# A convolution's last two groups of tokens: transformed while they are on chip, with two results put aside, instead of stored and loaded again

## The chip, the cores and the metric

The kernel runs on one core of a Trainium2 chip. The metric is the device time of one execution in microseconds (us). Three runs of the kernel before took 985.76, 987.46 and 989.23 us; the median, 987.46 us, is the time before. A profile is taken from one further execution.

The engines are named as in the profile: PE is TensorE's matrix multiplication and PEld its loading of weights, DVE is VectorE, ACT is ScalarE, POOL is GpSimd and SP is SyncE, which here only issues transfers (DMAs). ACTq, SPq and POOLq are the instruction queues of these engines where they issue a DMA. Every engine works through its own instructions in order, so an instruction that waits holds up all that stand behind it on the same engine.

## The reference

The computation is a "macaron" block on 2048 tokens of width 1024: half a feed-forward step, then a step of convolution and block-local attention, then half a feed-forward step again, each on normalised tokens and each added to its input. The change lies in the convolution:

```python
x = L0_attn_inputs                                   # (1, 2048, 1024), float32
x = x + 0.5 * ffn(layernorm(x))                      # router, sign weights
x = x + attn(layernorm(x))
x = x + 0.5 * ffn(layernorm(x))

# at the head of attn:
x = lax.conv_general_dilated(inputs, conv_w, window_strides=(1,), padding='SAME',
        dimension_numbers=('NWC', 'WIO', 'NWC')) + conv_b   # 3 taps, 1024 -> 768 channels
q, k, v = jnp.split(x, 3, axis=-1)                   # each 256 wide, then 16 heads of 64 in blocks of 128
```

## The kernel before

**Stages.** The first feed-forward step runs over 16 tiles of 128 tokens. It ends each tile with the normalised tokens of the next step, which TensorE transposes so that channels lie on partitions. Then comes the convolution, then attention, then the second feed-forward step.

**The convolution in eight points.** Three taps on runs of six outputs are computed with eight products instead of eighteen. From eight neighbouring inputs of each run, VectorE makes eight combinations, the points k = 0 to 7; from the three taps come eight combinations of weights; TensorE multiplies point k of the inputs by point k of the weights; and VectorE turns the eight products of a run into its six outputs. 2048 tokens are 342 runs of six. The tile `V[k]` holds point k of all 342 runs, with 8 chunks of 128 channels (DC = 8), so 8 x 342 columns. `product(w, k, ...)` (L528) multiplies one `V[k]` for one of six output chunks `w` of 128 channels. It is 8 matrix products in float32, which the trace shows as 16 instructions of line 520, and ScalarE copies its result out of the accumulator (L535, L537). Accumulators are four banks that the products take in turn.

**Groups.** Three token tiles make a group: 64 runs, or 512 columns of `V[k]` over the 8 chunks. There are six groups, n = 0 to 5 (TRIPLES = 6); the last has only 22 runs, 176 columns. The tokens of a group lie in a window tile of 1560 KB. There are two window buffers (`xwp`, L90ff.) while the feed-forward step runs. `transpose_x2` (L396) fills them in turn. When a group is complete, `end_transform` (L435, three instructions) makes points 0 and 7 from it, and `store_window` (L444) writes the window to memory outside the chip, since the buffer is wanted for a later group. Groups 4 and 5 are the last two and still lie in the two buffers when the feed-forward step ends. Their store is done in `conv_ends` (L551 to L553).

**Inner points.** Points 1 to 6 come in pairs (1,2), (3,4), (5,6), from `transform(n, k, ...)` (L454): six VectorE instructions for one group and one pair, two each for the sums over even and odd neighbours and two that combine them (L464 to L469). The memory has room for six `V` tiles at a time. So `V[1]` to `V[4]` are made during the products of points 0 and 7, in `conv_ends` (L539), and `V[5]`, `V[6]` take over the buffers of `V[0]` and `V[7]` when the products of these are done, in `last_transforms` (L568). The order of groups in `conv_ends` is the list `jobs` (L543): 4 and 5 from the buffers where they lie, then 0, 1, 2, 3, loaded again by `load_window` (L448) on ScalarE's queue; one transform goes beside each of the twelve products. In `last_transforms` the order is 1, 2, 3, 0, 4, 5, and while it runs the windows 0, 4 and 5 are loaded again. At most three windows are on chip at a time: two in `xwp`, one in `xs`.

**Weights.** The combinations of taps for points 1 to 6 are made by `taps_begin` (L491; loads on GpSimd's queue, one of them adding) and `taps_end` (L504; two VectorE instructions, L508 and L509) for each output chunk and pair. The first product of a pair needs line 508. For the first output chunk, `taps_end` for points 5 and 6 stands behind `last_transforms` (L731 to L733). The pinned instructions (`pin`) keep the order of the program among themselves; all others are put in an order by a planner that runs when the program is built, from estimated costs, and that order is what each engine follows.

**Behind it.** When the windows are done with (`wins.close()`, L732), three attention weights (L745) are loaded by SP into their memory. `outputs` (L583) turns the products of a chunk into the tile `y` (tag `y6`, 342 x 6 columns, one buffer), which is stored; it is first used after the first chunk's last product.

Of the kernel before, what the change touches and what calls it, by code (L numbers as in the profile page):

```python
# [9 lines left out]
F32 = mybir.dt.float32  # L10
# [7 lines left out]
P = 128  # L18
# [6 lines left out]
def kernel(  # L25
# [22 lines left out]
    nc = tc.nc  # L48
# [4 lines left out]
    NT = T // P  # L53
    DC = D // P
    NW = conv_w.shape[0]
# [8 lines left out]
    def pool(stack, name, bufs, **kw):  # L64
        return stack.enter_context(tc.tile_pool(name=name, bufs=bufs, reuse_waits="tile", **kw))

    const = pool(ctx, "const", 1)
    spill = pool(ctx, "spill", 1, space=DRAM)
# [4 lines left out]
    def bank(kind, shape, name):  # L73
        return banks[kind].tile(shape, F32, name=name, tag=kind)
# [14 lines left out]
    xwp = pool(wins, "xwp", 2, side="right")  # L89
# [261 lines left out]
    NK = 8  # L351
    SCALES = (1.0, -2.0 / 9, -2.0 / 9, 1.0 / 90, 1.0 / 90, 1.0 / 180, 1.0 / 180, 1.0)
    PAIRS = ((1, 2), (3, 4), (5, 6))
    QT = 3 * P // 6
    NQ = -(-T // 6)
    TRIPLES = -(-NT // 3)
    SIZES = [min(QT, NQ - n * QT) for n in range(TRIPLES)]
# [7 lines left out]
    ROW = QT + 1  # L365
    LEFT, RIGHT = 5 * ROW - 1, QT
    AT = (LEFT, *(j * ROW for j in range(6)), 1)
    win_dram = [spill.tile([P, DC, 6 * ROW], F32, name=f"win_{n}") for n in range(TRIPLES)]
    x2, x2ns, xws = {}, {}, {}
    V = {k: ve.tile([P, DC, NQ], F32, name=f"v_{k}", tag=f"v{k}") for k in (0, NK - 1)}  # L370

# [4 lines left out]
    def window(n):  # L376
        if n not in xws:
            xws[n] = xwp.tile([P, DC, 6 * ROW], F32, name=f"xw_{n}", tag="xw")
            if SIZES[n] < QT:

                rows6 = xws[n].rearrange("p c (k q) -> p c k q", q=ROW)
                nc.gpsimd.memset(rows6[:, :, :, SIZES[n] - 1 :], 0.0)
            else:
                nc.gpsimd.memset(xws[n][:, :, 2 * ROW - 1 :: ROW], 0.0)
            if n == 0:
                nc.gpsimd.memset(xws[n][:, :, LEFT : LEFT + 1], 0.0)
        return xws[n]
# [8 lines left out]
    def transpose_x2(t):  # L396
        xn = x2ns.pop(t)
        n, third = divmod(t, 3)
        xw = window(n)
        at = third * P  # L400

        head = -at % 6
        tail = (at + P) % 6
        for h in range(DC // 4):
            tr = bank("acc", [P, 4, P], f"tr2_{t}_{h}")
            for c in range(4):
                nc.tensor.transpose(tr[:, c, :], xn[:, ts(4 * h + c, P)], ident)  # L407
            rows6 = xw[:, 4 * h : 4 * h + 4, :].rearrange("p c (k q) -> p c k q", q=ROW)
            q, whole = (at + head) // 6, (P - head - tail) // 6
            copy = nc.scalar.copy  # L410
            copy(
                rows6[:, :, :, ds(q, whole)],
                tr[:, :, head : P - tail].rearrange("p c (q k) -> p c k q", k=6),
            )
            if head:
                copy(rows6[:, :, 6 - head : 6, q - 1], tr[:, :, 0:head])
            if tail:
                copy(rows6[:, :, 0:tail, q + whole], tr[:, :, P - tail : P])
        if third == 2 or t + 1 == NT:
            end_transform(n, 0)  # L420
        if third == 0 and n > 0:
            nc.gpsimd.tensor_copy(xws[n - 1][:, :, RIGHT : RIGHT + 1], xw[:, :, 0:1])
            if t + 1 < NT:
                store_window(n - 1)
        if t == NT - 3:
            window(TRIPLES - 1)
        if third == 2 and n + 1 < TRIPLES:
            nc.gpsimd.tensor_copy(window(n + 1)[:, :, LEFT : LEFT + 1], xw[:, :, LEFT + QT : LEFT + ROW])
    def tokens(xw, n):
        return [xw[:, :, ds(at, SIZES[n])] for at in AT]  # L430

    def columns(k, n):
        return V[k][:, :, ds(n * QT, SIZES[n])]

    def end_transform(n, k, pinned=False):  # L435
        d = tokens(xws[n], n)
        a, b, c, e = (d[0], d[2], d[4], d[6]) if k == 0 else (d[7], d[5], d[3], d[1])
        v = columns(k, n)
        kept = pin if pinned else lambda ins: None
        kept(nc.vector.tensor_tensor(v, c, b, ALU.subtract))  # L440
        kept(nc.vector.scalar_tensor_tensor(v, v, 5.25, a, ALU.mult, ALU.add))
        kept(nc.vector.tensor_tensor(v, v, e, ALU.subtract))  # L442

    def store_window(n, pinned=False):  # L444
        end_transform(n, NK - 1, pinned)
        nc.sync.dma_start(out=win_dram[n], in_=xws[n])

    def load_window(n, pl):  # L448
        xws[n] = pl.tile([P, DC, 6 * ROW], F32, name=f"xl_{n}", tag="xw")
        nc.scalar.dma_start(out=xws[n], in_=win_dram[n])  # L450

    VT = 3

    def transform(n, k, tf):  # L454

        _, d1, d2, d3, d4, d5, d6, _ = tokens(xws[n], n)
        a, b = columns(k, n), columns(k + 1, n)
        tmp = tf.tile([P, DC, QT], F32, name=f"vt_{n}_{k}", tag="vt", bufs=VT)[:, :, 0 : SIZES[n]]
        f, even, odd, last = {
            1: (-4.25, 1.0, 1.0, 1.0),  # L460
            3: (-5.0, 0.25, 4.0, 0.5),
            5: (-1.25, 4.0, 0.25, 2.0),
        }[k]
        nc.vector.scalar_tensor_tensor(a, d4, f, d2, ALU.mult, ALU.add)  # L464
        nc.vector.scalar_tensor_tensor(a, a, even, d6, ALU.mult, ALU.add)
        nc.vector.scalar_tensor_tensor(tmp, d3, f, d1, ALU.mult, ALU.add)
        nc.vector.scalar_tensor_tensor(tmp, d5, odd, tmp, ALU.mult, ALU.add)
        nc.vector.scalar_tensor_tensor(b, tmp, -last, a, ALU.mult, ALU.add)
        nc.vector.scalar_tensor_tensor(a, tmp, last, a, ALU.mult, ALU.add)  # L469
# [69 lines left out]
    def conv_ends(mp, tf, up, xs):  # L539

        jobs = [(TRIPLES - 2, 1, xwp), (TRIPLES - 1, 2, xwp), (0, 3, xs), (1,), (2,), (3,)]  # L543
        load_window(0, xs)
        begun = WORDER[0]
        taps_begin(begun, PAIRS[2], up)
        for at in range(2 * NW):
            last, i = divmod(at, NW)
            w = WORDER[i]
            product(w, last * (NK - 1), gs[w, 2 * last], mp)  # L550
            if at == 0:  # L551
                for n in (TRIPLES - 2, TRIPLES - 1):
                    store_window(n, True)  # L553
            if not last:
                load_g(w, 2)
                if w == begun:
                    taps_begin(w, PAIRS[0], up)
                    taps_begin(w, PAIRS[1], up)
            elif i == 0:
                load_g(w, 1)  # L560
            elif i < 4:
                load_g(WORDER[1], (1, 2, 0)[i - 1])
            n, *more = jobs[at // 2]
            transform(n, 1 + 2 * (at % 2), tf)
            if more and at % 2:
                load_window(*more)

    def last_transforms(tf, xs):  # L568
        for k in PAIRS[-1]:
            V[k] = ve.tile([P, DC, NQ], F32, name=f"v_{k}", tag=f"v{0 if k == 5 else NK - 1}")  # L570
        for n, *more in (
            (1, 0, xwp),
            (2, TRIPLES - 2, xwp),
            (3, TRIPLES - 1, xs),
            (0,),
            (TRIPLES - 2,),
            (TRIPLES - 1,),
        ):
            transform(n, 5, tf)
            if more:  # L580
                load_window(*more)

    def outputs(w, mp):  # L583
        m = ms[w]
# [114 lines left out]
    up = pool(b1, "up", 1)  # L699
    vm = pool(b1, "vm", 1)  # L700
    mp = pool(b1, "mp", 1)
    for k in range(1, 5):
        V[k] = vm.tile([P, DC, NQ], F32, name=f"v_{k}", tag=f"v{k}")
    xs = pool(wins, "xs", 1, side="right")
    tf = pool(wins, "tf", 1, side="right")
    conv_ends(mp, tf, up, xs)
    for ks in PAIRS[:2]:
        taps_end(WORDER[0], ks, up)

# [16 lines left out]
    for i, w in enumerate(WORDER):  # L726
        for ks in PAIRS:
            for k in ks:
                product(w, k, us[w][k], mp)
            if i == 0 and ks[0] == 1:  # L730
                last_transforms(tf, xs)  # L731
                wins.close()  # L732
                taps_end(w, PAIRS[-1], up)  # L733
            if ks[0] == 1 and i + 2 < NW:
                load_g(WORDER[i + 2], 1, 2, 0)
            if i + 1 < NW:
                taps_begin(WORDER[i + 1], ks, up)
            if ks is PAIRS[-1]:
                outputs(w, mp)
            if i + 1 < NW:  # L740
                taps_end(WORDER[i + 1], ks, up)
        if i == 1:
            aw = pool(b2, "aw", 1, side="right")
            qkv0 = pool(b2, "qkv0", 1, side="right")
            wv_sb, wq_sb, wk_sb = (load_rows(aw, a, n, HE) for a, n in ((wv, "wv_sb"), (wq, "wq_sb"), (wk, "wk_sb")))  # L745
# [277 lines left out]
```

## Time and profile before

| what | value |
|---|---|
| median of three runs | 987.46 us (985.76 to 989.23) |
| profiled execution | 990.02 us, span 988.1 us |
| busy share of the span: TensorE, VectorE, ScalarE, GpSimd | 97%, 66%, 41%, 26% |
| window stores (`win<-xw`) | 6 of 1560 KB, median 6.0 us to landing |
| window loads (`xl<-win`) | 7 of 1560 KB, 6.4 to 16.8 us, median 10.1 |
| loads of taps (`u<-in_conv_w_dram`) | 24 of 512 KB, median 5.9 us |
| products of points 0 and 7 | 200.9 to 259.8 us |
| products of points 1 to 6 | 260.1 to 433.8 us |

How to read it: a profile line for a group of instructions names the line of the kernel, the engine, the operation and, as out<-in, the tiles it writes and reads, then the count, the busy time, the mean duration, and the idle time of its engine just before it with what ended that idle time. `xw` is a window as the feed-forward step filled it, `xl` a window loaded again, `win` its copy outside the chip, `vt` the temporary of a transform, `v` a `V` tile, `g` a tap, `u` a combination of taps, `cv` an accumulator, `m` its copy. The shares are averages over the span; what a change inside the convolution does is read from the stretch from 200 to 300 us.

### The profile page before, as it was taken

To read this page: it belongs to the slowest core of one execution; us is meant where nothing else is said; L and a number is where in the kernel's file an instruction comes from. 1 tells how busy PE (TensorE), PEld (TensorE's weight loads), DVE (VectorE), ACT (ScalarE), POOL (GpSimd) and SP (SyncE) were. 2 spreads that over 40 slices of the span, in tenths; PEclk is the share of its full clock that TensorE was granted. 3 is DMA by queue.
4 is the path that set the end of the run, shared out by engine and by line. 5 is a ranking of instruction groups with operands and counts; after the bars stand their busy time and mean duration, and the time that the engine had idled before them with its cause. 6 is when DMAs were issued, how large, how long until landed. Compare 5 with 4: busy or idle time off the path is not lost.

```text
span 988.1 us, 13874 instructions
## 1 busy us (share of the span) xinstructions
PE 959.2 (97%) x5068; PEld 626.9 (63%) x5068; DVE 652.7 (66%) x1229; ACT 407.8 (41%) x1115; POOL 256.0 (26%) x327
## 2 busy tenths in 40 slices
PE   5999999999979999999999999999999999999998
PEld 3778887776646666654555455544554565878776
DVE  4878887786985656735656455645565655777764
ACT  3576665321011111125545344626462572545450
POOL 3554453320001101003303110311031322434331
PEclk9999999999989999999999999999999999999999
DMA  8766753599597675417030241025003236656431
GB/s 251 225 156 195 189 173 129 197 363 363 203 310 202 176 186 122 112 47 283 1 128 1 89 146 43 2 99 199 1 1 107 73 57 192 168 152 163 115 107 64
DMA packets 37396, 143.08 MB, mean 145 GB/s; under 512 B 4361, under 2 KB 5385, under 8 KB 34898
## 3 DMA queue, kind: packets, MB, share of 16 engines
q1 hardware_dynamic: 27760, 101.35, 28.4%
q0 software_dynamic: 8544, 29.64, 15.8%
q10 hardware_dynamic: 1026, 11.22, 3.0%
q8 instruction: 40, 0.66, 0.3%
q14 instruction: 26, 0.21, 0.1%
HBM read 84.37 MB, written 41.04 MB: 127 GB/s over the span
## 4 chain that ended last, share of the span: by engine, by line
PE 49%; issue 31%; DVE 9%; POOL 6%; DMA 4%; ACT 1%; POOLq 0%; SPq 0%; DVEq 0%; ACTq 0%
PE pm_f L287 22%; PE cv L520 11%; POOL xr L798 3%; PE tr_f L200 3%; PE pp L932 2%; DMA xl<-win 2%; POOL p L854 2%; PE lgp_f L208 2%; PE acc L913 2%; PE is_f L251 1%; DMA win<-xw 1%; PE tr L407 1%; PE pq L821 1%; PE ao L896 1%; DVE v L469 1%
## 5 line engine op out<-in xcount | busy, mean ns | idle before, releaser
L287 PE MATMUL pm_f<-sw,y_f 128*128 128x512 f32 x1024 | 265.6, 408 | 0.2 <-DVE x L297 0.2
L287 PEld LDWEIGHTS pm_f<-sw,y_f 128*128 128x128 f32 x1024 | 186.2, 191 | 40.7 <-DVE x L297 0.4
L520 PE MATMUL cv<-v,u 128*128 128x342 f32 x576 | 168.0, 454 | 6.0 <-DVE u L508 6.0
L520 PEld LDWEIGHTS cv<-v,u 128*128 128x128 f32 x576 | 109.8, 191 | 64.2 <-issue 8.2
L854 POOL TENSOR_SCALAR_AFFINE_SELECT p<-p 128x512 f32<-128x512 f32 x64 | 39.7, 645 | 282.9 <-ACT p L852 282.9
L867 ACT ACTIVATE p<-p,anm 128x128 f32<-128x128 f32 x256 | 99.0, 389 | 16.6 <-DVE anm L864 16.6
L265 POOL TENSOR_TENSOR y_f<-xnT_f,y_f 128x512 fp32r<-128x512 f32 x64 | 81.1, 1282 | 59.5 <-ACT y_f L264 58.8
L537 ACT ACTIVATE m<-cv 128x342 f32<-128x342 f32 x42 | 19.1, 456 | 169.7 <-PE cv L520 141.7
L852 ACT COPY p<-sc 128x512 f32<-128x512 f32 x64 | 34.3, 588 | 111.4 <-PE sc L842 111.3
L864 DVE TENSOR_REDUCE anm<-p 128x4 f32<-128x512 f32 x64 | 40.9, 681 | 49.0 <-POOL p L854 49.0
L296 DVE TENSOR_TENSOR pm_f<-pm_f,os_f 128x512 f32<-128x512 f32 x64 | 44.4, 694 | 35.0 <-PE pm_f L287 34.5
L913 PE MATMUL acc<-oT,wo_sb 128*128 128x512 f32 x128 | 67.2, 616 | 0.4 <-DVE oT L905 0.4
L821 PE MATMUL pq<-qkv,wq_sb 128*128 128x512 f32 x128 | 61.0, 596 | 0.0
L821 PE MATMUL pq<-qkv,wk_sb 128*128 128x512 f32 x128 | 60.2, 592 | 0.0
L520 PE MATMUL cv<-v,g 128*128 128x342 f32 (+2 forms) x224 | 57.1, 415 | 0.8 <-DVE v L442 0.8
L932 PE MATMUL pp<-pw_sb,o2T 128*128 128x512 f32 x128 | 57.4, 599 | 0.4
L805 PE MATMUL pv<-wv_sb,qkv 128*128 128x512 f32 x128 | 56.1, 592 | 0.0
L520 PEld LDWEIGHTS cv<-v,g 128*128 128x128 f32 x224 | 39.7, 190 | 17.6 <-DVE v L442 1.2
L201 ACT COPY xnT_f<-tr_f 128x512 f32<-128x512 f32 x60 | 32.6, 589 | 42.0 <-PE tr_f L200 42.0
L508 DVE SCALAR_TENSOR_TENSOR u<-g,u 128x1024 f32<-128x1024 f32 x18 | 22.0, 1224 | 41.5 <-issue 21.6
L867 ACT ACTIVATION_READ_ACCUMULATOR p<-p,anm 128x1 f32 x256 | 48.1, 188 | 0.0
L875 DVE TENSOR_TENSOR p<-p,asum 128x512 f32<-128x512 f32 x64 | 45.6, 712 | 2.2
(141 smaller groups left out, 1484.4 us busy)
## 6 DMA issues: line engine op xcount, KB each, us to landing
g<-in_conv_w_dram SPq DMA_DIRECT2D x28, 512.0 KB, 5.4
u<-in_conv_w_dram POOLq DMA_DIRECT2D x24, 512.0 KB, 5.9
xl<-win ACTq DMA_DIRECT2D x7, 1560.0 KB, 10.1
win<-xw SPq DMA_DIRECT2D x6, 1560.0 KB, 6.0
x<-in_x_dram SPq DMA_DIRECT2D x16, 512.0 KB, 4.5
raw<-in_weight_t_dram SPq DMA_DIRECT2D x16, 512.0 KB, 6.9
x<-hbias POOLq DMA_DIRECT2D x16, 512.0 KB, 5.2
x<-x SPq DMA_DIRECT2D x16, 512.0 KB, 5.1
```

Source lines behind the costliest of these rows:

```text
L265: nc.gpsimd.tensor_tensor(yl, y, yh.bitcast(F32), ALU.subtract)
L287: nc.tensor.matmul(pm, lhsT=y[:, n, c, :], rhs=self.sw[:, c, ts(h, NB)], start=(c == 0 and n == 0), stop=(c == DC - 1 and n == 1),)
L296: nc.vector.tensor_tensor(pm, pm, o, ALU.mult)
L520: nc.tensor.matmul(accs[w, k][:, lo:hi], lhsT=uk[:, c, :], rhs=V[k][:, c, lo:hi], start=(c == 0), stop=(c == DC - 1),)
L805: nc.tensor.matmul(pv, lhsT=qkvs[g][2][:, c, ts(b, P)], rhs=wv_sb[:, c, ts(half, NB)], start=(c == 0), stop=(c == WC - 1),)
L821: nc.tensor.matmul(pq, lhsT=w_sb[:, c, ts(hp, P)], rhs=qkvs[g][n][:, c, :], start=(c == 0), stop=(c == WC - 1),)
L854: nc.gpsimd.affine_select(out=p, in_=p, pattern=[[0, BPG], [-1, P]], compare_op=ALU.is_ge, fill=NEG_INF, base=0, channel_multiplier=1,)
L864: nc.vector.tensor_reduce(nmax, p, AX.X, ALU.max, negate=True)
L867: nc.scalar.activation(p[:, b, :], p[:, b, :], AF.Exp, bias=nmax[:, b : b + 1], accum_out=asum[:, b : b + 1],)
L875: nc.vector.tensor_tensor(p, p, asum.unsqueeze(2).broadcast_to([P, BPG, P]), ALU.mult)
L913: nc.tensor.matmul(accs[g][m], lhsT=wo_sb[:, hp, ts(m, P)], rhs=oT, start=(hp == 0), stop=(hp == NHP - 1),)
L932: nc.tensor.matmul(pp, lhsT=o2T[:, m, ts(b, P)], rhs=pw_sb[:, m, ts(h, NB)], start=(m == 0), stop=(m == WC - 1),)
```

## The change

Windows 4 and 5 are neither stored nor loaded again. All three pairs of inner points of these groups are made in `conv_ends`, while they lie in their buffers. As `V[5]` and `V[6]` have no memory yet, the two results of the third pair go into the tile `kept`, which uses the buffer of `y` (2 x 8 x 86 of its columns; 86 = 64 + 22 runs). `last_transforms` begins with a ScalarE copy of each of the two halves of `kept` into the last 86 runs of `V[5]` and `V[6]`, and then makes only groups 1, 2, 3 and 0. Window 0 is the only one that is loaded a second time, after group 1. The fourteen transforms of `conv_ends` are shared out over its twelve products.

```diff
+    KEPT = (TRIPLES - 2, TRIPLES - 1)
-    win_dram = [spill.tile([P, DC, 6 * ROW], F32, name=f"win_{n}") for n in range(TRIPLES)]
+    win_dram = [spill.tile([P, DC, 6 * ROW], F32, name=f"win_{n}") for n in range(KEPT[0])]
...
         if third == 0 and n > 0:
-            if t + 1 < NT:
+            if n - 1 not in KEPT:
                 store_window(n - 1)
...
-    def transform(n, k, tf):
+    def transform(n, k, tf, into=columns):
-        a, b = columns(k, n), columns(k + 1, n)
+        a, b = into(k, n), into(k + 1, n)
...
     def conv_ends(mp, tf, up, xs):
-        jobs = [(TRIPLES - 2, 1, xwp), (TRIPLES - 1, 2, xwp), (0, 3, xs), (1,), (2,), (3,)]
+        at0 = KEPT[0] * QT
+        y6 = mp.tile([P, NQ, 6], F32, name="kept", tag="y6", bufs=1).rearrange("p q j -> p (q j)")
+        kept = y6[:, 0 : 2 * DC * (NQ - at0)].rearrange("p (k c q) -> p k c q", k=2, c=DC)
+
+        def aside(k, n):
+            return kept[:, k - 5, :, ds(n * QT - at0, SIZES[n])]
+
+        jobs = [
+            *((n, k) for n in KEPT for k in (1, 3, 5)),
+            *((n, k) for n in range(KEPT[0]) for k in (1, 3)),
+        ]
+        loads = {(KEPT[0], 5): (1, xwp), (KEPT[1], 5): (2, xwp), (0, 3): (3, xs)}
         load_window(0, xs)
...
             if at == 0:
-                for n in (TRIPLES - 2, TRIPLES - 1):
-                    store_window(n, True)
+                for n in KEPT:
+                    end_transform(n, NK - 1, True)
...
-            n, *more = jobs[at // 2]
-            transform(n, 1 + 2 * (at % 2), tf)
-            if more and at % 2:
-                load_window(*more)
+            share = len(jobs) * at // (2 * NW), len(jobs) * (at + 1) // (2 * NW)
+            for n, k in jobs[slice(*share)]:
+                transform(n, k, tf, aside if k == 5 else columns)
+                if (n, k) in loads:
+                    load_window(*loads[n, k])
+        return kept

-    def last_transforms(tf, xs):
+    def last_transforms(tf, kept):
         for k in PAIRS[-1]:
             V[k] = ve.tile([P, DC, NQ], F32, name=f"v_{k}", tag=f"v{0 if k == 5 else NK - 1}")
-        for n, *more in ((1, 0, xwp), (2, TRIPLES - 2, xwp), (3, TRIPLES - 1, xs), (0,), (TRIPLES - 2,), (TRIPLES - 1,)):
+            nc.scalar.copy(V[k][:, :, KEPT[0] * QT :], kept[:, k - 5])
+        for n in (1, 2, 3, 0):
             transform(n, 5, tf)
-            if more:
-                load_window(*more)
+            if n == 1:
+                load_window(0, xwp)
...
-    conv_ends(mp, tf, up, xs)
+    kept = conv_ends(mp, tf, up, xs)
...
-                last_transforms(tf, xs)
+                last_transforms(tf, kept)
```

## The prediction

> **What bounds the kernel now.** First the page: span and busy shares, then the group of convolution products.
>
> ```profile
> span 988.1 us, 13874 instructions
> PE 959.2 (97%) x5068; PEld 626.9 (63%) x5068; DVE 652.7 (66%) x1229; ACT 407.8 (41%) x1115; POOL 256.0 (26%) x327
> L520 PE MATMUL cv<-v,u 128*128 128x342 f32 x576 | 168.0, 454 | 6.0 <-DVE u L508 6.0
> ```
>
> TensorE is busy for 97% of the span, so only its gaps and a low clock can be won back by moving other work. In the convolution it is idle for 6.0 us, all of it ended by VectorE's tap combination in line 508. I then asked for the stretches around these gaps (columns: length; busy time and count of PE, PEld, DVE, ACT, POOL; granted clock; DMA share; GB/s).
>
> ```profile
> 204.00:225.60 21.60, 20.75 (x102) 15.72 (x101) 21.58 (x47) 3.99 (x9) 3.25 (x5) 1.00 1.01 355
> 225.60:233.40 7.80, 7.80 (x29) 5.11 (x28) 0.02 (x1) 0.46 (x1) 0.00 (x0) 1.00 1.04 366
> 233.40:259.90 26.50, 26.36 (x92) 17.03 (x90) 26.41 (x43) 2.28 (x5) 0.00 (x0) 1.00 0.67 253
> 259.90:278.90 19.00, 18.67 (x64) 12.04 (x64) 19.00 (x31) 2.31 (x6) 1.41 (x2) 1.00 0.86 315
> 278.90:284.40 5.50, 0.00 (x0) 0.02 (x1) 5.29 (x13) 1.35 (x2) 0.86 (x1) 0.69 1.02 302
> 284.40:287.40 3.00, 2.98 (x6) 1.83 (x6) 2.90 (x3) 0.00 (x0) 0.00 (x0) 0.50 1.07 294
> ```
>
> From 204 to 284 VectorE is full except for one hole, 225.6 to 233.4; TensorE's hole, 278.9 to 284.4, is at the end of the same stretch. Here VectorE sets the pace, and its early hole is paid back as TensorE's late one. The row after it shows a second price: the clock is 0.50 until 287.4. The chain that ended last says what made VectorE's hole (start, length, what):
>
> ```profile
> 208.19 13.71 DMA win<-xw
> 221.91 0.04 ACTq L450
> 221.95 0.04 issue
> 221.99 11.47 DMA xl<-win
> 233.48 0.69 DVE v L464
> ...
> 271.26 8.37 DMA xl<-win
> 279.63 0.02 issue
> 279.65 0.34 DVE v L464
> ```
>
> Group 1 cannot be loaded until group 4, whose buffer it takes, has been stored: 13.71 us of store, then 11.47 us of load. Group 5's reload (8.37 us) is on the chain too, though VectorE waits only 0.17 us for it, because other work fills in. The timeline of TensorE and of the last tap combination closes the picture:
>
> ```profile
> 260.14 18.67 PE L520 MATMUL cv<-v,u 128*128 128x342 f32 x64 [0.38 <-DVE u L508]
> 283.05 1.22 DVE L508 SCALAR_TENSOR_TENSOR u<-g,u 128x1024 f32<-128x1024 f32 x1
> 284.42 16.00 PE L520 MATMUL cv<-v,u 128*128 128x342 f32 x49 [5.61 <-DVE u L508]
> ```
>
> **The change, part by part.** I write (n,k) for the transform of group n for points k and k+1.
>
> *Removed.* Two stores on SP and two reloads on ScalarE's queue (groups 4, 5), 1560 KB each, and with the stores the 13.71 us ahead of group 1's load. SP only issues g loads behind the stores; these may start 0.9 us earlier, worth nothing by itself. ScalarE loses two reload waits on VectorE (at 267.05 and 271.26) that had evictions behind them.
>
> *Moved.* (4,5) and (5,5) go from the tail to the front. A 512-column instruction of VectorE follows another by 0.60 us on the chain, a 176-column one by 0.25 us: 6 x 0.60 + 6 x 0.25 = 5.1 us. They fall where VectorE has its 7.9 us hole. Without that cover the 5.1 us would be neither gain nor loss, since the same 5.1 us leave the tail.
>
> *Added.* Two ScalarE copies of 8 x 86 = 688 columns. No row has this size; ScalarE's 342-column eviction takes 0.456 us and its 1024-column multiply (L501) 1.05, so the line through them gives 0.76 us each. Bounds: 0.59 (the 512-column copy) and 1.05. I take 0.76. The second one waits for V7's buffer, that is for the last k=7 product at 259.6. Behind it on ScalarE stand evictions of the last k=7 and first k=1, 2 products and perhaps the second load of group 0. Four accumulator banks at 4.56 us a product leave an eviction 13.7 us; in the trace one waited 9.96 us behind a window load and TensorE did not stop. Cost: 0; without this cover, each us of ScalarE is one of TensorE.
>
> *VectorE's new sum*, from 204.62 (first end transform of group 4) to the first k=5 taps: ends 5.1; (4,·) and (5,·) with k=1, 3, 5: 3 x 3.62 + 3 x 1.51 = 15.4; (0,1), (0,3) 7.2; six transforms of groups 1 to 3: 21.7; four tap combinations of 1.14: 4.6; (1,5), (2,5), (3,5), (0,5): 14.5; the k=5 taps 1.1. Together 69.6, so 274.2 if nothing waits. The planner ran four 0.43 us instructions of the output step ahead of these taps before; if it does so again, 275.9. (Check on before: 69.6 + 1.7 + the waits 7.86 + 0.17 = 79.3, against 79.65 from 204.62 to 284.27.)
>
> *Do the loads arrive?* Group 1 is issued when (4,5) has read its buffer, about 220.5, and needed when (0,3) is done, 232.3. Before, it took 11.5 us beside two stores: 232.0, no wait. Group 2: issued about 225.1, needed 239.5; between 10.3 and its 16.8 of before, a wait of 0 to 2.8 us. Group 3: needed 246.8, issued 231.7, 10.3: no wait. Group 0 again: issued when (1,5) has read, 261.0, needed 269.5; the load issued at 260.63 before took 7.5 us, the median is 10.1: a wait of 0 to 1.6 us. The Trainium skill ("DMA: Bandwidth & Descriptors", Queues, rings and completion order) speaks against hoping for more: every DMA engine takes the queue rows in turn, packet by packet, so that SP's g loads and POOL's u loads keep halving a window load although the stores are gone. From the page's 358 GB/s and its fixed 2 us I estimate 6.5 us for a load alone and 11 at half rate; the rows (7.5 to 16.8) agree with the second, and I use the rows. Sum of the waits: 0 to 4.4, so VectorE is done between 274.2 and 280.3. I take about 276.5, the nearer end, as each load has slack.
>
> *TensorE.* The last k=7 matmul starts at 259.3; starts are 0.285 us apart, so k=1 can start at 259.6 (its taps are now ready about 255; before, 260.14). Four products are 64 starts, 18.2 us: k=5 is wanted at 277.8. VectorE's 276.5 is earlier, so TensorE doesn't stop. Won: 284.42 - 277.83 = 6.6 us. And the clock: six starts took 2.98 us at 0.50 where 6 x 0.285 = 1.7 would do, 1.3 us. Here a page speaks against me: "TensorE: Matmul & The Clock Gate", Part 1, has a free-running window of about 3.4 us and says of the ramp "don't fit to a specific cold count"; without the 1.3 the gain would be 6.6. I keep it: the row has it in the profiled execution, and where there is no gap there is no ramp to vary. The same page makes a rest of a stall under one window free of clock loss; the trace agrees as far as it goes (the 0.38 us gap at 259.8 left the clock at 1.00).
>
> *Does it last?* From 287 to 988 the waits of TensorE that the profile names add up to 3.5 us, so what follows simply starts earlier. What is late next would be the second output chunk's taps: its u load starts at 268.9 when k=2 is done, a second accumulates (5.3 + 5.9 us, median; up to 13.5 for one), taps 2.3, against a need at 277.8 + 9.1 = 286.9. The three weight loads (1024 KB each) that wait for the windows' memory come at about 272 instead of 275.5 to 286.4 and crowd these u loads, but 3.2 MB of reloads have left the same stretch: 283 to 285, in time.
>
> Sum: 6.6 + 1.3 = 7.9 us. The profiled execution lasted 990.02 us (span 988.1): 982.1. It lay 2.6 us above the median of the runs; on the median, 987.46 - 7.9 = **979.6 us**.
>
> **The rivals.**
>
> *Part of the stall stays.* The waits for groups 2 and 0 add up and the output instructions go first: k=5 starts 1 to 3 us late, at 980.6 to 982.6, and over 3.4 us with the clock's 1.3 on top, up to 984.5. For it: only 1.3 to 3.6 us of slack on VectorE. Against: every load was costed with before's traffic. About 982.
>
> *The hole only moves: no change.* ScalarE issues group 1's load behind an eviction, or the planner puts an instruction that needs a load ahead of work that doesn't, as it did at 233.48 (group 1's first instruction stood ahead of three of (0,3)). Then VectorE idles some 8 us elsewhere and ends at 284 as before: 987. Against: 28 us of VectorE's work now stand ahead of the first needed load.
>
> *Slower: the second load of group 0.* Its place is the end of VectorE's tail, where (0,5) and the k=5 taps, 4.8 us, have to follow it; ScalarE, its issuer, may hold it behind the copy of V6 and an eviction. It decides at a landing of 279.7 (284.42 - 4.8): later than that is slower than before, one for one. Issued at 264.6 behind the k=1 eviction, the longest landing of before (16.8) gives 281.4; behind the k=2 eviction (269.2) it gives 286: 994. With a median landing these are 274.7 and 279.3, still faster. Price taken: about 991.
>
> **How the numbers follow.** Forecast 0.65, part of the stall 0.17, no change 0.08, slower 0.10. Within 0.3% (3 us, about what a measurement of this kernel can tell from no change) lies above 984.5. Faster 0.65 + 0.15 = 0.80; same 0.08 + 0.02 = 0.10; slower 0.10. Range: below, 6.6 + 1.3 plus the 0.85 us that TensorE waits at 209.85 and the spread of the medians (1.7): 977. Above, the partly stalled case with 1 us of spread: 985.5; this leaves out about 0.18 above and little below.
>
> **What would show it.** VectorE's wait for a load of a window falls from 8.0 us to under 3; the store of windows is x4 and the load x5; TensorE has no gap of over 1 us between 204 and 300, and no row at 0.50 there; k=5 of the first chunk starts near 278; the two copies take about 0.76 us. The forecast is wrong if TensorE still waits for line 508 at k=5, if evictions hold it up behind ScalarE's queue, or if the second chunk's taps come late.

## The result, and the profile after

The changed kernel takes 979.38 us (median of six runs, 977.1 to 981.14), the kernel before 986.61 us in six runs beside it. The ratio is 0.9921, with a 95% interval of 0.9894 to 0.9949: 7 us faster. The forecast was 979.6 us. That the two agree to 0.2 us is in part luck: the forecast was taken off a median of three runs, 987.46 us, and six runs have 986.61.

The profiled execution lasted 980.25 us, with a span of 978.0 us. First the page of the kernel after: span, busy shares and the group of the convolution's products, as in the prediction.

```profile
span 978.0 us, 13872 instructions
PE 955.0 (98%) x5068; PEld 624.4 (64%) x5068; DVE 652.0 (67%) x1229; ACT 409.4 (42%) x1117; POOL 256.1 (26%) x327
L521 PE MATMUL cv<-v,u 128*128 128x342 f32 x576 | 166.0, 450 | 0.0
```

The last number of the third line was 6.0 us, ended by the taps of line 508. It is 0.0: nothing stops these products any more. Their mean duration fell from 454 to 450 ns because none of them runs at the low clock. Next the stretches of the same numbers as before; the convolution begins 1.9 us earlier in this execution, so each holds slightly later work (length; busy time and count of PE, PEld, DVE, ACT, POOL; granted clock; DMA share; GB/s).

```profile
204.00:225.60 21.60, 20.75 (x100) 15.39 (x99) 21.57 (x51) 4.11 (x9) 2.46 (x4) 1.00 0.95 276
225.60:233.40 7.80, 7.80 (x29) 5.13 (x28) 7.48 (x13) 1.57 (x3) 0.00 (x0) 1.00 1.01 411
233.40:259.90 26.50, 26.50 (x94) 17.42 (x93) 26.50 (x42) 3.39 (x7) 0.00 (x0) 1.00 0.57 200
259.90:278.90 19.00, 19.00 (x68) 12.49 (x67) 15.40 (x25) 2.86 (x5) 2.27 (x3) 1.00 0.64 213
278.90:284.40 5.50, 5.50 (x21) 3.63 (x20) 3.21 (x4) 0.46 (x1) 0.01 (x1) 1.00 1.04 320
284.40:287.40 3.00, 3.00 (x12) 1.92 (x12) 2.97 (x7) 1.40 (x2) 0.14 (x1) 1.00 1.01 336
```

In the second row VectorE is busy for 7.48 us where it was busy for 0.02. In the fifth TensorE is busy for all of 5.50 us where it did nothing. In the sixth the clock is 1.00 where it was 0.50. The hole has left VectorE and the stop has left TensorE with it. The timeline of the kernel after gives the two instructions that meet there, then the chain of waits what is left of VectorE's wait for a window (total, times, longest):

```profile
257.72 42.49 PE L521 MATMUL cv<-v,u 128*128 128x342 f32 x147
272.52 1.22 DVE L509 SCALAR_TENSOR_TENSOR u<-g,u 128x1024 f32<-128x1024 f32 x1
```

```profile
DVE v L465 <- DMA xl<-win: 0.3, 1, 0.3
```

The products of points 1 to 6 run without a break. The taps that the first k=5 product needs are ready at 273.7. The product wants them 64 starts of 0.285 us after 257.7, at 275.9 (worked out, since no break shows where it starts). So VectorE has 2.2 us to spare.

**Where the time went.** I take as the length of the convolution the time from its first product to the first value product of the attention. It was 433.6 - 201.1 = 232.5 us and is 423.6 - 199.2 = 224.4 us: 8.1 us less. Behind it, both spans have 554.4 or 554.5 us. Ahead of it the two profiled executions differ by 1.9 us, in a stretch that the change doesn't touch. In the execution before, the granted clock was 0.86 from 35 to 40 us and 0.80 from 40 to 45 us, some 3.4 us at half speed and at most 1.7 us lost; in the one after it was 1.00 there. The other versions' profiles, all with the change or most of it, start between 197.7 and 199.6 us. One profile of the kernel before can't show whose these 1.9 us are; that the medians differ by 7.2 us, and the spans, which hold them, by 10.1, speaks against the change.

### The profile page after: what moved, and what is told of

Its sections match the earlier page's. It is cut to its first block, busy times and chain, and to the rows that moved or that the text cites. A ratio compares the mean times of both kernels' runs of the same rounds, so it can differ in the third digit from the quotient of the medians.

```text
span 978.0 us, 13872 instructions
## 1 busy us (share of the span) xinstructions
PE 955.0 (98%) x5068; PEld 624.4 (64%) x5068; DVE 652.0 (67%) x1229; ACT 409.4 (42%) x1117; POOL 256.1 (26%) x327
## 4 chain that ended last, share of the span: by engine, by line
PE 45%; issue 26%; POOL 5%; DVE 1%; DMA 0%; ACT 0%; POOLq 0%; DVEq 0%
PE cv L521 22%; PE pm_f L287 13%; POOL xr L807 3%; PE pp L941 2%; POOL p L863 2%; PE acc L922 2%; PE tr_f L200 1%; PE pq L830 1%; PE lgp_f L208 1%; PE is_f L251 1%; PE ao L905 1%; PE pt L892 1%; PE sc L851 0%; DMA qkv<-y 0%; DVE y L618 0%
## 5 line engine op out<-in xcount | busy, mean ns | idle before, releaser
L521 PE MATMUL cv<-v,u 128*128 128x342 f32 x576 | 166.0, 450 | 0.0
L876 ACT ACTIVATE p<-p,anm 128x128 f32<-128x128 f32 x256 | 99.0, 389 | 16.8 <-DVE anm L873 16.8
```

The source lines that it names most:

```text
L521: nc.tensor.matmul(accs[w, k][:, lo:hi], lhsT=uk[:, c, :], rhs=V[k][:, c, lo:hi], start=(c == 0), stop=(c == DC - 1),)
L876: nc.scalar.activation(p[:, b, :], p[:, b, :], AF.Exp, bias=nmax[:, b : b + 1], accum_out=asum[:, b : b + 1],)
```

## The experiments

The times of one version scatter by several us. The length of the convolution is steadier: the changed kernel and two other versions without a stop, each in one profile, all have 224.4 us. So the experiments are read by that length, by TensorE's stop ahead of the first k=5 product, and by VectorE's waits for windows.

**All four transfers put back, the transforms left where the change put them.**

```diff
...
                 for n in KEPT:
                     end_transform(n, NK - 1, True)
+                    nc.sync.dma_start(out=win_dram[n], in_=xws[n])
...
             if n == 1:
                 load_window(0, xwp)
+            if n == 2:
+                load_window(KEPT[0], xwp)
+            if n == 3:
+                load_window(KEPT[1], xs)
```

> The changed kernel with all four removed transfers put back: the two stores of windows 4 and 5, and in the tail their two loads, which nothing reads. The transforms stay where the change put them. The length of the convolution (first product of point 0 to first value product of the attention) was 232.5 us before and 224.4 us after. Theory A, VectorE's hole is what counted and it now has work to cover it: group 1's load is issued when the stores have landed, about 220 instead of 217.8, VectorE waits 0 to 3 us for it, and its slack of 2.2 us before the k=5 products takes that up: length 224.4 to 225.5, time 979 to 981. Theory B, the traffic of these 6.4 MB slowed the other loads: most of the gain is lost, length 228 to 232.5, time 983 to 987.

Measured: 981.76 us (ratio 0.9918, 0.9887 to 0.9949); length 422.9 - 198.2 = 224.7 us. No stop. The chain of waits of this run:

```profile
DVE v L465 <- DMA xl<-win: 2.3, 1, 2.3
```

Group 1's load waits for the stores again, and VectorE for the load: 2.3 us instead of 0.3. The slack of 2.2 us takes up the 2.0 us more. So it is not the 6.4 MB as such that made the kernel before slow. The stores could have stayed, as long as VectorE has work beside them.

**Only group 4 kept; group 5 stored and loaded again.**

```diff
...
                 for n in KEPT:
                     end_transform(n, NK - 1, True)
+                    if n == 5:
+                        nc.sync.dma_start(out=win_dram[n], in_=xws[n])
...
-            *((n, k) for n in KEPT for k in (1, 3, 5)),
+            *((n, k) for n in KEPT for k in ((1, 3, 5) if n == 4 else (1, 3))),
...
-        for n in (1, 2, 3, 0):
+        for n in (1, 2, 3, 0, 5):
             transform(n, 5, tf)
...
+            if n == 2:
+                load_window(5, xwp)
```

The two copies cover group 4's 64 runs alone, and group 2's load follows (5,3).

> Half of the change: only group 4 is kept on chip and its third pair put aside; group 5 is stored and loaded again as before. Theory A (the store ahead of group 1's load made the hole): the hole is gone, and VectorE's tail is 1.5 us longer by (5,5), which its slack of 2.2 us takes: length of the convolution 224.4 to 225.2, the whole gain, time about 979.5. Theory B (each group counts by the work and the bytes that it takes from the tail): group 4 is 3.6 of 5.1 us, so some 70% of the gain: 226.9, time about 981.7.

Measured: 978.65 us (ratio 0.9901, 0.9875 to 0.9926); length 422.7 - 198.3 = 224.4 us. The chain of waits of this run:

```profile
DVE v L465 <- DMA xl<-win: 1.5, 1, 1.5
```

TensorE doesn't stop. Group 4 alone brings the whole gain.

**Only group 5 kept; group 4 stored and loaded again.** The same edit with 4 and 5 exchanged; group 1's load then follows (4,3).

> The other half: only group 5 is kept; group 4 is stored and loaded again. Theory A: group 1's load stands behind a store again, though a single one (8 to 10 us instead of 13.7), so VectorE's hole is 0 to 2 us, and the tail is 3.6 us longer by (4,5): TensorE stops for 1.5 to 4 us at the first k=5 product. Length 226 to 229, time 981 to 984.5. Theory B (by work and bytes, 30% of the gain): 230.1, time 985.

Measured: 980.92 us (ratio 0.9932, 0.991 to 0.9955); length 424.2 - 199.1 = 225.1 us. The chain of waits and the timeline of this run:

```profile
DVE v L465 <- DMA xl<-win: 2.6, 1, 2.6
...
PE cv L521 <- DVE u L509: 0.5, 1, 0.5
```

Both expectations are missed, and mine (226 to 229) for a reason worth keeping: I counted (4,5) as 3.6 us more in the tail and forgot that the same 3.6 us then leave the front. VectorE's work up to the k=5 taps is the same in every version; only its waits differ. By waits alone: 2.6 - 0.3 = 2.3 us, and 0.4 us for an output instruction that the planner put ahead of the taps, less the 2.2 us of slack, gives a stop of 0.5 us, which is what is there. The hole shrank from 7.9 to 2.6 us although group 1's load still follows a store: one store instead of two is ahead of it, and the load was issued 17.8 us after the convolution's first product, in the kernel before 20.9 us. So the gain is not the sum of two halves. Either half takes away most of the hole, and what is left of it fits, or all but fits, into the slack.

**The second load of group 0 issued late** (the rival that ends on the slower side).

```diff
-            if n == 1:
-                load_window(0, xwp)
+            if n == 3:
+                load_window(0, xs)
```

> The changed kernel with the second load of group 0 issued after (3,5) instead of after (1,5), into that window's buffer. This is the rival of the late load. Theory A: issued near 266 it lands near 274 to 276, (0,5) and the k=5 taps follow in 4.8 us, so the first k=5 product starts at 278.5 to 281 instead of 275.9: length 227 to 230.5, and at a gap of over 3.4 us part of the clock's 1.3 us on top. If the load had slack to spare, length 224.4.

Measured: one time, 987.03 us; length 430.3 - 198.4 = 231.9 us. The timeline of this run, then its stretches around the restart:

```profile
274.45 0.69 DVE L465 SCALAR_TENSOR_TENSOR v<-xl 128x512 f32<-128x512 f32 x1 [4.25 <-DMA xl<-win]
...
279.99 20.27 PE L521 MATMUL cv<-v,u 128*128 128x342 f32 x60 [4.41 <-DVE u L509]
```

```profile
278.87:279.99 1.12, 0.00 (x1) 0.03 (x1) 1.12 (x2) 0.00 (x0) 0.00 (x0) 0.50 0.90 282
279.99:285.70 5.71, 5.71 (x10) 3.50 (x11) 5.21 (x6) 0.00 (x0) 0.00 (x0) 0.51 0.97 245
```

Then TensorE alone (length; busy time and count of PE; granted clock; DMA share; GB/s):

```profile
285.00:286.00 1.00, 1.00 (x4) 0.72 1.01 385
```

The stop, 4.4 us, is within what I expected. But the length is 7.5 us longer, not at most 6. The last view shows why: a granted clock of 0.72 from 285 to 286 is 0.56 us at half and the rest at full, so the clock stays at half until 285.6, 5.6 us after the restart, which loses 2.8 us. In the kernel before, a longer stop of 5.6 us was followed by only 3.4 us at half clock. The shorter stop cost nearly as much, 7.2 against 7.3 us. The load landed just ahead of 274.45; on the kernel before's time (its convolution began 2.6 us later) that is 277.1, and of the gain 0.6 us are left. The rival decides about 2 us earlier than the 279.7 that I gave: the output instructions ahead of the taps and the clock were not in that figure.

**Spare work on VectorE.** To find the slack and the price of a stop, instructions whose results nobody uses are put ahead of the k=5 taps: three, six, eight or fourteen. Here the three; the others have `range(5)`, `range(7)` and `range(13)`.

```diff
...
+        spare = tf.tile([P, DC, QT], F32, name="spare", tag="vt", bufs=VT)
+        pin(nc.vector.tensor_tensor(spare, kept[:, 0, :, 0:QT], kept[:, 1, :, 0:QT], ALU.add))
+        for _ in range(2):
+            pin(nc.vector.scalar_tensor_tensor(spare, kept[:, 0, :, 0:QT], 0.5, kept[:, 1, :, 0:QT], ALU.mult, ALU.add))
```

> The changed kernel with three extra VectorE instructions (0.60 us apart, results unused) in front of the k=5 taps of the first chunk. They make VectorE 1.8 us later there. Theory A says it has 2.2 us to spare (its taps end at 273.7, the product wants them at 275.9), so TensorE doesn't stop: length of the convolution 224.4 to 224.8. A theory in which TensorE's time follows VectorE's chain one for one says 226.2.

> The changed kernel with six extra VectorE instructions (3.6 us) ahead of the k=5 taps; the planner puts two output instructions (0.43 us each) ahead of them as well, so the taps come 4.5 us later and TensorE stops for 2.4 us. This is the stop that is shorter than a clock window of 3.4 us. If such a stop costs only itself: clock 1.00 throughout, length of the convolution 226.8. If the clock falls for it too (the stops of 3.7 and 4.4 us lost a further 2.9 each): 228 to 230.

> The same with eight extra instructions, 4.8 us. Theory A: TensorE stops for 2.6 us at the first k=5 product, which is under one clock window of 3.4 us, so the clock stays at 1.00: length 227.0. If a stop costs clock in proportion to its length (1.3 us for 5.6), 227.6.

> The same with fourteen extra instructions, 8.4 us. Theory A: a stop of 6.2 us. The clock falls to half, and how much of the low stretch lies after the restart depends on where its windows happen to lie: 1.3 us were lost in the kernel before (5.6 us stop), 2.9 with the late load of group 0 (4.4 us stop). Length 224.4 + 6.2 + 0.5 to 3.4: 231.1 to 234. With no price for the clock, 230.6.

Measured (one time each: 977.69, 983.51, 985.25 and 992.03 us), with the other versions for comparison. "Low clock" is the part of the half-clock stretch, by the granted clock, that lies after the restart; half of it is lost.

| version | stop of TensorE, us | low clock after it, us | stop + loss, us | length, us |
|---|---|---|---|---|
| after | 0 | 0 | 0 | 224.4 |
| three spare | 0 | 0 | 0 | 224.4 |
| only group 5 | 0.5 | 0 | 0.5 | 225.1 |
| six spare | 2.0 | 0 | 2.0 | 226.6 |
| eight spare | 3.7 | 6.1 | 6.8 | 231.4 |
| group 0 late | 4.4 | 5.6 | 7.2 | 231.9 |
| before | 5.6 | 3.4 | 7.3 | 232.5 |
| fourteen spare | 9.9 | 4.5 | 12.1 | 236.7 |

The table rests on stretches like these two, from the restart on: first of the run with six spare instructions, then of the run with eight (the clock is the third number from the end):

```profile
278.71:285.00 6.29, 6.29 (x22) 4.22 (x23) 4.20 (x5) 0.46 (x1) 0.60 (x1) 1.00 1.04 315
```

```profile
278.87:284.70 5.83, 5.83 (x10) 3.51 (x11) 4.11 (x5) 0.00 (x0) 0.00 (x0) 0.50 1.04 325
```

Six microseconds of products are 22 instructions in the first and 10 in the second. Next, where the half-clock stretch ends: in the run with eight, in the kernel before (0.61 from 287 to 288: half until 287.8), and in the run with fourteen:

```profile
285.00:286.00 1.00, 1.00 (x5) 1.00 1.04 426
```

```profile
287.00:288.00 1.00, 1.00 (x4) 0.61 1.04 274
```

```profile
286.11:290.60 4.49, 4.49 (x8) 2.83 (x9) 4.38 (x5) 0.00 (x0) 0.00 (x0) 0.50 0.35 120
290.60:292.00 1.40, 1.40 (x6) 0.92 (x5) 1.30 (x2) 0.00 (x0) 0.00 (x0) 1.00 0.00 0
```

The loss can also be read without the clock, from ScalarE's copy of the first k=5 product, which waits for its last instruction. Here it is with six and with eight spare instructions, and in the kernel before:

```profile
283.59 0.46 ACT L538 ACTIVATE m<-cv 128x342 f32<-128x342 f32 x1 [5.44 <-PE cv L521]
```

```profile
286.77 0.46 ACT L538 ACTIVATE m<-cv 128x342 f32<-128x342 f32 x1 [10.20 <-PE cv L521]
```

```profile
290.96 0.46 ACT L537 ACTIVATE m<-cv 128x342 f32<-128x342 f32 x1 [10.71 <-PE cv L520]
```

Counted from the restarts (278.71, 278.87 and 284.42) that is 4.88, 7.90 and 6.54 us: 3.0 and 1.7 us lost, as in the table. The lengths exceed 224.4 us by 0.2 to 0.3 us more than stop and loss; in the kernel before by 0.8 us, of which 0.5 us is the later start of its k=1 products.

Three spare instructions cost nothing. With the output instructions that went along, the taps came 2.2 us later than in the changed kernel, the whole slack. So the slack is real, and TensorE's time does not follow VectorE's chain one for one. With eight and fourteen the stop was larger than I had worked out (3.7 and 9.9 us against 2.6 and 6.2): the planner put output instructions of 0.43 us between the spare ones, ahead of the taps. So both lengths lie above everything expected of them, and the run with eight no longer tests a short stop. The run with six does; two such instructions were foreseen there, and its stop of 2.0 us is near the 2.4 expected.

**A third chunk's product begun early.**

```diff
     product_columns(WORDER[1], 0, gs[WORDER[1], 0], 0, FIRST)
+    product_columns(WORDER[2], 0, gs[WORDER[2], 0], 0, FIRST)
```

> A further version, meant to beat both: a third output chunk's product of point 0 begins on the first 256 columns, ahead of the last group's points (two do so before and after the change). It is to fill the 0.85 us that TensorE waits for group 5's point 0. The split costs 16 more instructions; if the 256-column and the 86-column half run at their own pace, 0 to 0.3 us. Length 223.5 to 224.4, time 978.5 to 979.4, not to be told from the changed kernel by its time; if the split costs more than the wait, up to 225.

Measured: 979.3 us (ratio 0.9926, 0.9904 to 0.9948); length 422.6 - 198.7 = 223.9 us. The 0.85 us wait for group 5's point 0 is gone from the chain of waits and the length is 0.5 us less. Its time can't be told from that of the changed kernel.

## Why the prediction was right

- **Which resource sets the pace.** As forecast, VectorE's early hole was TensorE's late stop. The versions above vary the hole from 0.3 us (after) over 1.5, 2.3 and 2.6 to 8.0 us (before). Up to 2.3 us TensorE doesn't stop, since beyond the 0.3 us VectorE has 2.2 us of slack; at 2.6 it stops for 0.5 us, at 8.0 for 5.6.
- **The hole's cause.** The prediction named the store ahead of group 1's load. That is right for the kernel before, but the store need not go: with the transfers put back the length stays at 224.7 us. What the change does is to put 5.1 us of work ahead of the point where VectorE waited, and to start the load earlier: 18.6 us after the first product instead of 20.9 us. With the transfers put back it started at 20.1 us, so the work by itself was enough; the earlier load without the work was not run.
- **The moved 5.1 us.** They run between 213.4 and 225.3 us, in the front, as the prediction had it. VectorE's work from the first end transform of group 4 to the k=5 taps took 202.74 to 273.66, 70.9 us, against 69.6 and the 1.7 us of output instructions: two of these four went ahead of the taps.
- **The loads.** Five of them, 7.7 to 10.4 us, against 6.4 to 16.8 before. VectorE waited 0.3 us in all, the low end of the 0 to 4.4 us (4.0 by the prediction's own numbers: group 2 issued at 225.1 and 16.8 us long is 2.4 us late, not 2.8). No load took the 11 us estimated for half rate; the fastest before, 6.4 us, is about the 6.5 estimated for a load alone. That estimate is a loose one: the page's fixed 2 us is a fit for transfers issued by GpSimd, these are ScalarE's, and one stretch shown above moved 411 GB/s by the profile's count, more than the 358 it used. The prediction's sum used the rows, so nothing rests on it.
- **The two copies.** 0.757 and 0.758 us against 0.76 from the line through two rows. No eviction that stood behind them held up a product.
- **The stop.** 6.6 us were forecast for the start of the k=5 products. Counted from the first product of the convolution it moved from 83.4 to 76.8 us: 6.6.
- **The clock.** 1.3 us were counted, against the page that says not to fit such a count. The low stretch of the kernel before lasted until 287.8, not 287.4, and cost 1.7 us. So the amount was 0.4 us short for this pair of kernels, and that it was so near was luck: 2.2 to 3.1 us were lost in the versions with a stop of 3.7, 4.4 and 9.9 us. In the rivals, where I priced a rest of the stop at 1.3 us on top, it was undersized by up to 1.8. The 1.3 and 2.9 us named in the expectation for fourteen spare instructions are 1.7 and 2.8 by this measure.
- **What follows.** The first of the second chunk's taps was done at 282.4, 2.6 us ahead of its product at 285.0 (275.9 + 9.1). The second was done at 284.0 and is wanted one product later. On the time of the kernel before, 284.0 is 285.9, 0.9 us past the 283 to 285 of the prediction. Nothing was late, but this is the nearest margin after the k=5 taps. The three weight loads were issued at 270.6, 271.1 and 278.2 us, where about 272 was forecast; whether they slowed these taps was not tried.
- **The sum.** 7.9 us forecast; 8.1 us in the convolution's length, 7.2 us between the medians. From the median of six runs the same sum would have said 978.7.

## What to carry to other kernels

Follow an engine's hole forward to where another engine stops: a wait of 8 us on an engine that is 66% busy can cost the bound engine 5.6 us fifty microseconds later, because in between the first engine has no slack. When work is moved into such a hole, count both ends: what arrives at one place leaves the other, and only the waits change the sum. And measure the slack with a few spare instructions. It says how much of a change was needed; here, half of it.

## What the runs showed of the hardware

The price of a stop of TensorE has a step. Stops of 0.5 and 2.0 us left the granted clock at 1.00 and cost themselves. A stop of 3.7 us cost 6.8 us, nearly as much as one of 5.6 us (7.3). The clock fell 2.1 to 4.1 us after the stop began, and in the traces' record of the granted clock the low stretch was 6.83 us long after stops of 3.7, 4.4 and 5.6 us and 10.24 us after the one of 9.9 us: two or three times 3.41 us. What is lost is half of the part that lies after the restart, so a longer stop can lose less: 2.2 us after the stop of 9.9, 3.1 after that of 3.7. This fits the free-running window of about 3.4 us of the Trainium skill ("TensorE: Matmul & The Clock Gate", Part 1), and the numbers here are what it makes of a single stop in the middle of a kernel. Where exactly between 2.0 and 3.7 us the step lies was not tried, and with a free-running window it need not be one value.
